# A graph-attention layer on one core: where the steps of a background MLP pass stand among the attention's steps, and how its last groups are cut

## The chip, the cores and the metric

The kernel runs on one core of one Trainium2 chip. The metric is device time in microseconds, the median of three runs. Engines are named as in the profile: PE is TensorE (matmul; PEld its weight load), DVE is VectorE, ACT is ScalarE, POOL is GpSimd, SP is SyncE.

## The reference, cut to what matters

Two residual layers over 6250 nodes of 512 numbers and 100000 edges; an edge takes the key and value of its node `dst` to its node `src`.

```python
x = x + gnn(layernorm(x), [src, dst], edge_attr)     # attention over edges, 8 heads of 64
x = x + ffn(layernorm(x)[None])[0]                    # a small "ALU" per node

# gnn: rows = src, cols = dst of every edge
q, k, v = x @ Wq + bq, x @ Wk + bk, x @ Wv + bv
logits = einsum('ehd,ehd->eh', q[rows] * scale, k[cols]) + att_bias
p = exp(logits - segment_max(logits, rows)[rows])
y = segment_sum(p / segment_sum(p, rows)[rows] * v[cols], rows)
out = y @ Wo + bo

# ffn: decode nibbles of the normalised row, run two three-layer MLPs (160 wide,
# relu after the first two) on them, add one-hot results into columns 128 to 160
```

## The kernel before, in words

A first stage sorts the edges by `src`, normalises the nodes and writes the keys and values of all nodes to DRAM (`kv_d`). The change touches the main loop, which starts some 490 us into the span.

The nodes are sorted by degree and cut into 49 blocks of 128, taken in the order of the list `ORDER`. Block b has `CAP[ORDER[b]]` slots, one slot being one edge of each of its 128 nodes: 34 in the first block, then large and small ones in turn (25, 11, 24, 11, ... 18, 14, ... 16, 16), 10, 9 and 8 in the last three, 804 in all. A block of more than 12 slots is handled in two parts (three in the first two blocks), with a running softmax. Blocks are written here by number and part, 25.1 being the second part of block 25.

A part goes in steps of two slots. For each step:

- GpSimd gathers the keys and values of each slot (`gather`, L110, `kv<-kv_d,rec`) into one of 11 buffers of two slots (`kvp`, `bufs=11`), and, running ahead, the edge records (`rec<-rec_d,eid`): some four gathers a step.
- `pump()` advances background work by one piece: every generator in the list `going`, and the first one in the list `alus`.
- `dots` (L801, L802): VectorE multiplies the keys by the block's queries and sums over each head.
- At the first step of a part, the weighted sum of the *previous* part is issued (`sums`): per step `weigh` multiplies the values by the softmax weights (on VectorE, L812; the second of four on ScalarE in 16 instructions, L810), and TensorE adds the slots up by matmuls with the identity (L1077), two for each slot. These matmuls are the last readers of a `kv` buffer.

After the last step of a part, `softmax` runs on VectorE (L730 to L738), with the exponential on ScalarE (L739); `total` (L754) needs it next.

The list `going` holds a block's own follow-up: `project` (the next block's queries, L790 to L797) and `part_end`, which rescales and adds the part sums (L1041, L1045), divides (L773 to L777), and runs `attend_out`: transposes (L820) and their copy (L823), output projection (L829), and three pumps later the residual and its statistics (L834 to L837, the tile `x1`).

The list `alus` holds the ALU passes of the second layer. A pass covers a group of blocks, four (`GB`) but for the last ones. Its generator `alu` stops (yields) after each of 20 pieces: the root (L842), normalise (L844 to L854), decode (L860 to L873), the transposes `pf` (L878), their copy `fT` (L882), five matmuls of the first layer each with its relu (pm3, L893 and L895), five of the second (pm4, L906 and L908; the fifth sums five weights, the others two), the third layer (p3, L913), a pause, its copy `yf` with a transpose (L917, L921), a pause, and the end (L928 to L963). Finished blocks are scattered to the output by GpSimd (L782).

The program is written under a manual schedule: each engine's queue has the order in which the code issues the instructions. So the place of a `pump()` in the loop is the place of the piece's instructions in the queues of TensorE, ScalarE and VectorE. After the last block, pumps run until nothing is left.

Before, each step has one pump, ahead of its dot products; the weighting of blocks 45 to 48 has one more after every second buffer; the groups are eleven of four blocks (0 to 43), then 44 and 45, 46 and 47, and 48 by itself.

Of the kernel before, what the change touches and what calls it, by code (L numbers as in the profile page):

```python
# [13 lines left out]
AF = mybir.ActivationFunctionType  # L14
# [14 lines left out]
GB = 4  # L29
# [14 lines left out]
def gnn_ffn_kernel(  # L44
# [3 lines left out]
    nc = tc.nc  # L48
# [7 lines left out]
    NB = -(-N // P)  # L56
# [17 lines left out]
    def ctile(shape, name, dt=F32, pool=const):  # L74
        return pool.tile(shape, dt, tag=name, name=name)
# [12 lines left out]
    eps = ctile([P, 1], "eps")  # L88
    nc.vector.memset(eps, EPS)
    warm = ctile([P, 1], "warm")  # L90
# [18 lines left out]
    def gather(dst_t, table, idx):  # L109
        nc.gpsimd.indirect_dma_start(  # L110
            out=dst_t, out_offset=None, in_=table,
            in_offset=bass.IndirectOffsetOnAxis(ap=idx, axis=0))
# [107 lines left out]
    def fetch_keys(b):  # L220
        C = CAP[ORDER[b]]
        t, nbuf = ("0", 1) if b == 0 else ("", LA + 3)
        kg = pre.tile([P, C + 1], F32, tag="kg" + t, name="kg", bufs=nbuf)
        gather(kg, words, pos_i[:, ORDER[b]:ORDER[b] + 1])
        st[b] = dict(kg=kg)
# [18 lines left out]
    def fetch_recs(n, last):  # L244

        while fetched[0] < n and fetched[1] is not None and fetched[1][0] <= last:
            b, s = fetched[1]
            gather(st[b]["rec"][:, s, :], rec_d, st[b]["eid"][:, s:s + 1])
            fetched[:] = fetched[0] + 1, next(wanted, None)
# [501 lines left out]
    def total(lg, cor, den0):  # L751

        den = ap_.tile([P, H], F32, tag="den", name="den", bufs=3)
        nc.vector.tensor_reduce(den, lg.rearrange("p c h -> p h c"), AX.X, OP.add)  # L754
        if cor is not None:
            nc.vector.tensor_tensor(den0, den0, cor, op=OP.mult)
            nc.vector.tensor_tensor(den, den, den0, op=OP.add)
        return den
# [40 lines left out]
    def dots(kvt, n, q, dot, s):  # L799
        k = kvt[:, :n, :D]  # L800
        nc.vector.tensor_tensor(k, k, q[:, None, :].to_broadcast([P, n, D]), op=OP.mult)  # L801
        nc.vector.tensor_reduce(  # L802
            dot[:, s:s + n, :], k.rearrange("p s (h d) -> p s h d", h=H), AX.X, OP.add)

    def weigh(kvt, n, p, p_ps, s, on_act):
        v = kvt[:, :n, D:].rearrange("p s (h d) -> p s h d", h=H)
        if on_act:
            for i in range(n):
                for h in range(H):
                    nc.scalar.mul(v[:, i, h], v[:, i, h], p[:, s + i, h:h + 1])  # L810
        else:
            nc.vector.tensor_tensor(  # L812
                v, v, p_ps[:, s:s + n, :, None].to_broadcast([P, n, H, DK]), op=OP.mult)
# [156 lines left out]
    def fetch_nodes(b):  # L970
        if b - 4 in ends:
            run(ends.pop(b - 4))
        xg = ap_.tile([P, 2 * D], F32, tag="xg", name="xg", bufs=4)
        gather(xg, xx_d, nid[:, b:b + 1])
        st[b]["xg"] = xg


    going = []
    alus = []
# [8 lines left out]
    def store(n=1):  # L988
        for _ in range(n):
            stores.pop(0)[1]()  # L990

    def pump():
        last[1] += 1
        for g in list(going) + alus[:1]:
            if next(g, True):
                for l in (going, alus):
                    if g in l:
                        l.remove(g)
        if stores and stores[0][0] + last[0] <= last[1]:
            store()  # L1000

    def run(g):

        while alus and g in alus and g is not alus[0]:
            run(alus[0])
        for _ in g:
            pass
        for l in (going, alus):
            if g in l:
                l.remove(g)  # L1010
# [8 lines left out]
                LASTR if ORDER[g + j] == NB - 1 else P), g))  # L1019


    heads_of = list(range(0, NB - 5, GB)) + [NB - 5, NB - 3, NB - 1]
    head = {b: max(g for g in heads_of if g <= b) for b in range(NB)}

    def start_group(g):
        i = heads_of.index(g)
        n = (heads_of + [NB])[i + 1] - g
        t, nbuf = ("", 2) if i < len(heads_of) - 2 else (str(i), 1)
        if i > 1 and nbuf > 1 and heads_of[i - 2] in groups:
            run(groups.pop(heads_of[i - 2])[2])  # L1030
            while stores and stores[0][2] <= heads_of[i - 2]:
                store()
        groups[g] = [o2.tile([P, n if t else GB, D], F32, tag="x1" + t, name="x1", bufs=nbuf),
                     o2.tile([P, GB, 2], F32, tag="mv", name="mv", bufs=4), None]

    def part_end(b, i, parts, p_y, cor, den):
        yield
        s_ = st[b]
        if i:
            y = s_["y"]  # L1040
            nc.vector.tensor_tensor(y, y, cor[:, :, None].to_broadcast([P, H, DK]), op=OP.mult)  # L1041
        yield
        yield
        if i:
            nc.vector.tensor_tensor(y, y, heads(p_y), op=OP.add)  # L1045
        else:
            y = s_["y"] = o2.tile([P, H, DK], F32, tag="y", name="y", bufs=2)
            if parts > 1:
                nc.scalar.copy(y, heads(p_y))
        if i < parts - 1:  # L1050
            return
        some = divide(y, y if i else heads(p_y), den, p_y)
        yield
        g = head[b]
        if g == b:
            start_group(g)
        x1, mv, _ = groups[g]
        for _ in attend_out(y, some, s_["xg"], x1[:, b - g], mv[:, b - g]):
            yield
        del st[b]  # L1060
        if b == NB - 1 or head[b + 1] != g:
            groups[g][2] = group_end(g, b - g + 1)
            alus.append(groups[g][2])
# [5 lines left out]
    def sums(b, i, parts, dot, cor, p_ps, kvs, n_):  # L1069
        s_ = st[b]  # L1070
        den = s_["den"] = total(dot, cor, s_.get("den"))

        p_y = ops.tile([P, D], F32, tag="p_y", name="p_y")
        for k, (kvt, n, s) in enumerate(kvs):
            weigh(kvt, n, dot, p_ps, s, k % 4 == 1)
            for j in range(n):
                nc.tensor.matmul(p_y, ident, kvt[:, j, D:], start=(s + j == 0),  # L1077
                                 stop=(s + j == n_ - 1))
            if b > NB - 5 and k % 2:
                pump()  # L1080
        ends[b] = part_end(b, i, parts, p_y, cor, den)
        going.append(ends[b])

# [2 lines left out]
    for b in range(NB):  # L1086
        C = CAP[ORDER[b]]
        s_ = st[b]
        rec, q = s_["rec"], s_["q"]
        parts = -(-C // PART)  # L1090
        m = None
        for i in range(parts):
            s0, s1 = C * i // parts, C * (i + 1) // parts
            n_ = s1 - s0
            dot = ap_.tile([P, n_, H], F32, tag="dot", name="dot", bufs=2)
            kvs = []
            for s in range(s0, s1, 2):
                n = min(2, s1 - s)
                kvt = kvp.tile([P, 2, 2 * D], F32, tag="kv", name="kv")
                for k in range(n):  # L1100
                    gather(kvt[:, k, :], kv_d, rec[:, s + k, 0:1].bitcast(I32))
                kvs.append((kvt, n, s - s0))
                done = sum(SLOTS[:b]) + s + n
                if done > HOLD:
                    last[0] = 1000
                fetch_recs(FIRST + (TOTAL - FIRST) * done // (TOTAL - LAST), b + LA)
                if s == s0 and i == 0:
                    if b + LA + 2 < NB:
                        fetch_keys(b + LA + 2)
                    if b + 1 < NB:  # L1110
                        fetch_nodes(b + 1)
                if s == s0 + 2 and i == 0 and b + 1 < NB:
                    pj = project(st[b + 1]["xg"], st[b + 1])
                    going.insert(0, pj)
                pump()
                dots(kvt, n, q, dot, s - s0)
                if s == s0:
                    for f in waiting:
                        f()
                    waiting.clear()  # L1120
                if s == s0 + 2 and i == parts - 1 and b + LA + 2 < NB:
                    read_keys(b + LA + 2)
            m, cor, p_ps = softmax(dot, rec[:, s0:s1], s_["neg"][:, s0:s1], m)
            waiting.append(partial(sums, b, i, parts, dot, cor, p_ps, kvs, n_))
        if b + 1 < NB:
            run(pj)
    for f in waiting:
        f()
    last[0] = 0
    while going or alus or stores:  # L1130
        pump()
# [145 lines left out]
```

## Time and profile before

| what | value |
|---|---|
| median of three runs | 2687.78 us (2687.76 to 2688.94) |
| profiled execution | 2684.3 us, its span 2682.4 us |
| mean granted TensorE clock | 0.864 |
| busy: PE, PEld, DVE, ACT, POOL | 1988.2, 862.5, 2018.2, 884.8, 1710.2 us |
| DMA | 542.31 MB, 202 GB/s over the span |

Times inside the profiled execution are counted from the start of its span. In a timeline's line stand the start, the duration, the engine, the line of the kernel, the operation, the tile written and the tiles read, and in brackets the idle time of that engine just before it with what ended that idle time. In a line of waits stand the waiting instruction, what it waited for, and the total, the count and the longest. In a table of stretches stand the stretch, its length, busy time and instructions of PE, PEld, DVE, ACT and POOL, the granted TensorE clock, the share of the DMA engines and GB/s.

### The profile page before, as it was taken

What the parts mean: (1) busy time and instruction counts of PE and PEld (TensorE: products, weight loads), DVE (VectorE), ACT (ScalarE), POOL (GpSimd) and SP (SyncE); (2) the same over time, 40 slices, a digit from 0 to 9 for tenths busy, and PEclk for the clock granted to TensorE, in tenths of its full rate; (3) what the DMA queues carried; (4) which work ended last, traced back from release to release, by engine and by line L of the source; (5) the groups of instructions that cost most, each with busy time, mean ns of one, the idle gap of its engine ahead of it and who ended that gap; (6) DMA issues with size and microseconds to landing.
All of it is one profiled execution on the core that took longest, in us unless ns stands there. A gap on an engine that the chain in (4) does not pass through costs nothing.

```text
span 2682.4 us, 20184 instructions
## 1 busy us (share of the span) xinstructions
PE 1988.2 (74%) x4853; PEld 862.5 (32%) x4853; DVE 2018.2 (75%) x3562; ACT 884.8 (33%) x2712; POOL 1710.2 (64%) x1857
## 2 busy tenths in 40 slices
PE   7888799256567658677786677867778777787775
PEld 3444344122223223332332223323333323333333
DVE  9899600469677787878879779798888978889762
ACT  6434242123233233232333323333233232333322
POOL 3011177767777677777776767777777777777610
PEclk9999899678788879888898798988889888898886
DMA  8545244566675667777776767767777777777710
GB/s 279 193 132 185 88 145 128 187 204 217 228 238 190 204 217 233 222 227 223 226 226 201 225 205 228 229 218 229 221 225 229 223 227 229 231 230 233 229 63 20
DMA packets 193965, 542.31 MB, mean 202 GB/s; under 512 B 51831, under 2 KB 53174, under 8 KB 193841
## 3 DMA queue, kind: packets, MB, share of 16 engines
q0 software_dynamic: 154416, 464.27, 55.2%
q1 hardware_dynamic: 39425, 76.67, 8.2%
q8 instruction: 42, 0.69, 0.1%
q14 instruction: 82, 0.67, 0.1%
HBM read 472.60 MB, written 68.22 MB: 202 GB/s over the span
## 4 chain that ended last, share of the span: by engine, by line
PE 35%; DVE 32%; POOL 12%; issue 10%; DMA 6%; ACT 3%; SPq 0%; DVEq 0%; POOLq 0%; ACTq 0%
PE p_y L1077 19%; POOL rec L110 7%; DVE kv L801 7%; DVE dot L802 6%; PE pm L906 4%; DVE kv L812 4%; PE pm L829 4%; POOL kv L110 3%; DMA kv<-kv_d,rec 3%; DVE key L143 3%; DVE key L144 2%; PE pm L457 2%; DMA rec<-rec_d,eid 2%; PE q L796 2%; ACT kv L810 2%
## 5 line engine op out<-in xcount | busy, mean ns | idle before, releaser
L1077 PE MATMUL p_y<-kv,ident 128*128 128x512 f32 x1608 | 849.2, 686 | 458.9 <-DVE kv L812 403.9
L110 POOL DMA_INDIRECT kv<-kv_d,rec x804 | 760.6, 946 | 293.0 <-issue 195.5
L110 POOL DMA_INDIRECT rec<-rec_d,eid x804 | 763.6, 950 | 245.1 <-issue 224.4
L1077 PEld LDWEIGHTS p_y<-kv,ident 128*128 128x128 f32 x1608 | 345.0, 222 | 951.3 <-DVE kv L812 459.4
L801 DVE TENSOR_TENSOR kv<-kv,q 128x1024 f32<-128x1024 f32 (+1 forms) x425 | 490.0, 1153 | 207.2 <-PE q L797 110.3
L802 DVE TENSOR_REDUCE dot<-kv 128x16 f32<-128x1024 f32 (+1 forms) x425 | 493.8, 1162 | 20.0
L810 ACT ACTIVATE kv<-kv,dot 128x64 f32<-128x64 f32 x1648 | 402.6, 335 | 0.2 <-DMA kv<-kv_d,rec 0.2
L812 DVE TENSOR_TENSOR kv<-kv,pp 128x1024 f32<-128x1024 f32 (+1 forms) x317 | 346.9, 1151 | 0.0
L796 PE MATMUL q<-wq,xT 128*128 128x512 f32 x392 | 186.8, 620 | 22.0 <-ACT xT L792 22.0
L829 PE MATMUL pm<-wo,yT 128*128 128x512 f32 x392 | 184.1, 614 | 10.5 <-ACT yT L823 10.5
L457 PE MATMUL pm<-wv,xnT 128*128 128x512 f32 (+1 forms) x392 | 186.9, 617 | 0.0
L457 PE MATMUL pm<-wk,xnT 128*128 128x512 f32 (+1 forms) x392 | 180.0, 600 | 0.0
L792 ACT COPY xT<-tr 128x512 f32<-128x512 f32 x49 | 28.7, 585 | 444.9 <-PE tr L790 444.9
L468 ACT COPY kvt<-pm 128x512 f32<-128x512 f32 (+1 forms) x98 | 56.9, 583 | 235.0 <-PE pm L457 160.4
L739 ACT ACTIVATE dot<-dot 128x64 f32<-128x64 f32 (+6 forms) x91 | 23.7, 260 | 309.0 <-DVE dot L738 308.9
L782 POOL DMA_INDIRECT out_dram<-x,nid x49 | 50.1, 1022 | 114.1 <-issue 77.5
L110 POOL DMA_INDIRECT kg<-sorted_d,pos_i x49 | 47.0, 960 | 110.9 <-DVE ov L699 96.3
L796 PEld LDWEIGHTS q<-wq,xT 128*128 128x128 f32 x392 | 72.8, 195 | 114.6 <-issue 77.1
L829 PEld LDWEIGHTS pm<-wo,yT 128*128 128x128 f32 x392 | 75.0, 196 | 102.7 <-issue 86.3
L895 ACT ACTIVATE h<-pm,b 128x512 f32<-128x512 f32 (+2 forms) x70 | 44.2, 632 | 185.8 <-PE pm L893 185.8
L143 DVE TENSOR_TENSOR key<-key 128x512 f32<-128x512 f32 x143 | 101.6, 710 | 4.8
L823 ACT COPY yT<-tr 128x512 f32<-128x512 f32 x49 | 28.5, 583 | 231.7 <-PE tr L820 231.7
(253 smaller groups left out, 2022.2 us busy)
## 6 DMA issues: line engine op xcount, KB each, us to landing
kv_d<-kvt SPq DMA_DIRECT2D x48, 512.0 KB
rec<-rec_d,eid POOLq DMA_INDIRECT x804, 3.5
kv<-kv_d,rec POOLq DMA_INDIRECT x804, 5.2
xt<-in_x_dram SPq DMA_DIRECT2D x48, 256.0 KB
xx_d<-xt SPq DMA_DIRECT2D x48, 256.0 KB
xx_d<-xn SPq DMA_DIRECT2D x48, 256.0 KB
rec_d<-R SPq DMA_DIRECT2D x3, 882.0 KB
bt<-in_edge_attr_dram SPq DMA_DIRECT2D x3, 686.0 KB
```

The costliest lines, as they stand in the source:

```text
L110: nc.gpsimd.indirect_dma_start(out=dst_t, out_offset=None, in_=table, in_offset=bass.IndirectOffsetOnAxis(ap=idx, axis=0))
L143: nc.vector.tensor_tensor(ov[:, :, 0, :], av[:, :, 0, :], av[:, :, 1, :], op=OP.min)
L457: nc.tensor.matmul(pm[:r], xnT[b][:, c, :r], wkv[nm_][:, c, :], start=(c == 0), stop=(i == 1 and c == KC - 1))
L468: nc.scalar.copy(kvt[:r, i * D:(i + 1) * D], pm[:r])
L796: nc.tensor.matmul(q, xT[:, c, :], wq[:, c, :], start=(c == 0), stop=False)
L801: nc.vector.tensor_tensor(k, k, q[:, None, :].to_broadcast([P, n, D]), op=OP.mult)
L802: nc.vector.tensor_reduce(dot[:, s:s + n, :], k.rearrange("p s (h d) -> p s h d", h=H), AX.X, OP.add)
L810: nc.scalar.mul(v[:, i, h], v[:, i, h], p[:, s + i, h:h + 1])
L812: nc.vector.tensor_tensor(v, v, p_ps[:, s:s + n, :, None].to_broadcast([P, n, H, DK]), op=OP.mult)
L829: nc.tensor.matmul(pm, yT[:, c, :], wo[:, c, :], start=(c == 0), stop=False)
L906: nc.tensor.matmul(pm[:, :nt], w, h1[:, k, :nt], start=(i == 0), stop=(i == len(terms) - 1))
L1077: nc.tensor.matmul(p_y, ident, kvt[:, j, D:], start=(s + j == 0), stop=(s + j == n_ - 1))
```

## The change

- `pump` takes a number n: the first ALU pass is advanced n times, the list `going` still once.
- In the main loop n is 0 at the last step of a part, 2 at its second step, 1 elsewhere.
- In the last three blocks (46 to 48) there is one more pump after the dot products of each step but the first.
- The pumps inside the weighting are gone.
- The last groups are 40 to 43, 44 and 45, and 46 to 48 (the single block 48 has no pass of its own).
- One more root of a dummy tile on ScalarE stands before the last weighting (`warm`).

```diff
-    def pump():
+    def pump(n=1):
+
         last[1] += 1
-        for g in list(going) + alus[:1]:
+        for g in list(going) + (alus[:1] * n):
             if next(g, True):
...
-    heads_of = list(range(0, NB - 5, GB)) + [NB - 5, NB - 3, NB - 1]
+    heads_of = list(range(0, NB - 5, GB)) + [NB - 5, NB - 3]
...
-        t, nbuf = ("", 2) if i < len(heads_of) - 2 else (str(i), 1)
+        t, nbuf = ("", 2) if i < len(heads_of) - 1 else (str(i), 1)
...
                 nc.tensor.matmul(p_y, ident, kvt[:, j, D:], start=(s + j == 0),
                                  stop=(s + j == n_ - 1))
-            if b > NB - 5 and k % 2:
-                pump()
...
-                pump()
+
+                pump(0 if s + 2 >= s1 else 2 if s == s0 + 2 else 1)
                 dots(kvt, n, q, dot, s - s0)
+                if b > NB - 4 and s > s0:
+                    pump()
...
             run(pj)
+    nc.scalar.activation(warm, eps, AF.Sqrt)
     for f in waiting:
         f()
```

## The prediction

> **What bounds the kernel now.** I read the page's busy table first, then the table of stretches of the main loop, the waits of GpSimd and VectorE there, and the timelines around the waits that the change moves.
>
> ```profile
> PE 1988.2 (74%) x4853; PEld 862.5 (32%) x4853; DVE 2018.2 (75%) x3562; ACT 884.8 (33%) x2712; POOL 1710.2 (64%) x1857
> ```
>
> ```profile
> 1060.00:1560.00 500.00, 362.83 (x839) 151.23 (x839) 411.44 (x690) 157.74 (x525) 372.92 (x393) 0.85 0.71 222
> 1560.00:2060.00 500.00, 380.07 (x886) 158.32 (x885) 427.95 (x742) 164.45 (x549) 372.77 (x392) 0.87 0.71 222
> 2540.00:2682.00 142.00, 94.18 (x287) 50.12 (x285) 60.37 (x163) 38.47 (x105) 14.97 (x15) 0.79 0.14 48
> ```
>
> No engine looks full. But GpSimd's gathers start 1.25 us apart (0.95 busy, 0.30 issue), so 393 of them are 491 of the 500 us. GpSimd sets the pace up to its last key/value gather at 2556; 126 us follow without it.
>
> ```profile
> 1411.94 0.95 POOL L110 DMA_INDIRECT xg<-xx_d,nid  x1 [0.30 <-DVE dg L955]
> 1420.34 0.94 POOL L110 DMA_INDIRECT kv<-kv_d,rec  x1 [7.45 <-PE p_y L1077]
> ```
>
> It is late only where it waits for one of the 11 kv buffers to be freed by the weighted-sum matmuls (L1077). Gaps above 0.5 us between 600 and 2540 come to 34.5 us; the largest are 8.4 (at 894), 7.45 (1420), 4.5 (1570), 3.3 (707). Each follows a late VectorE, whose own waits in this stretch are:
>
> ```profile
> DVE den L754 <- ACT dot L739: 91.8, 18, 9.3
> DVE fT L882 <- PE pf L878: 49.2, 8, 8.5
> DVE yf L917 <- PE p L913: 37.1, 4, 12.1
> DVE x L834 <- PE pm L830: 27.5, 11, 3.9
> ```
>
> VectorE is busy 82 to 86% from 1060 to 2060 and hardly waits for gathers there, so a new VectorE wait is paid once the ring's slack is gone. I measure the slack as the time between a buffer's last matmul and the gather that refills it. Its low points: 0.3 at 1758 (a wait already), 4.8 at 1926, 10.0 at 2097, 2.3 at 2260, 2.0 at 2427.
>
> **The change, part by part.** Parts are written block.part, steps counted from 1. An ALU pass has 20 pieces: root, normalise, decode, pf, fT, five pm3, five pm4, p3, pause, yf, pause, end. I wrote out which piece falls on which step, before and after. Pieces per part stay the same away from the end; only their places move: none at a part's last step, two at its second. The second step comes right after the weighting, so TensorE then has a burst of 12 to 24 matmuls queued, and whatever VectorE wants from TensorE there waits for the burst.
>
> *Softmax waits (gain).* The exponential queues on ScalarE behind the last relu of the part. In three-step parts (14.0, 18.0) that relu now stands ahead of the next q projection: 3.7 us less of 5.9 and 6.1; the waits of 2.9 and 3.2 in the parts after them go. In 22.0, 38.0, 42.0: 0.8 less. In 22.1, 38.1, 42.1 it waits for a pm4 of two weights (1.7 us) instead of five (4.3): 2.5 less. In 26.0, 30.0, 34.0: 0.8 less. In 26.1, 30.1, 34.1 one more two-weight pm4 is queued ahead: 1.7 more.
>
> *fT in groups 20, 24, 28 (cost).* Before, pf was at 25.1 step 1, ahead of the burst, and fT at step 2 found it done. Now both are at step 2, behind the burst and behind block 24's output projection (L829), which the same step issues first.
>
> ```profile
> 1663.68 1.01 PE L878 MATMUL pf<-ident,ft 128*8 128x128 f32 x4 [4.12 <-ACT yT L823]
> 1666.32 10.98 PE L1077 MATMUL p_y<-kv,ident 128*128 128x512 f32 x18 [1.62 <-DVE kv L812]
> 1677.13 3.60 PE L829 MATMUL pm<-wo,yT 128*128 128x512 f32 x8
> 1680.57 0.38 PE L830 MATMUL pm<-bo,sT 66*128 66x512 bf16 x1
> ```
>
> ```profile
> 1669.04 0.67 DVE L882 COPY fT<-pf 8x512 f32<-8x512 f32 x1
> 1680.98 0.69 DVE L834 TENSOR_TENSOR x<-pm,xg 128x512 f32<-128x512 f32 x1 [3.35 <-PE pm L830]
> ```
>
> fT was ready at 1669.0. It would come at 1680.95 + 0.8 for pf, 12.7 later, with the step's dot products (three pairs of 2.4 us) and the later steps queued behind it; x1 then comes at 1681.8 + 0.7 + 7.3 = 1689.8 instead of 1681.0. Net 8.8 per group (the fT waits that stand behind a burst already, 4.3 to 8.5 with one pair of 2.4 in between, would give 3.4 to 7.6; I take the group's own rows), and with the softmax terms 8.8 - 0.8 + 1.7 = 9.7.
>
> *yf in groups 16, 32, 36 (cost).* p3 moves from the first step of 23.0, 39.0 and 43.0 to the second.
>
> ```profile
> 2224.14 3.70 PE L906 MATMUL pm<-h,w1ml 128*128 128x512 f32 x8 [0.78 <-ACT h L908]
> 2229.48 4.46 PE L913 MATMUL p<-h,w 128*8 128x512 f32 x10 [0.78 <-ACT h L908]
> 2233.87 7.13 PE L1077 MATMUL p_y<-kv,ident 128*128 128x512 f32 x16
> ```
>
> The five-weight pm4 then takes p3's place ahead of the burst. The relu that released the pm4 at 2224.1 comes 1.7 later, one two-weight pm4 more being queued: pm4 to 2230.3 and its relu to 2230.9, ScalarE's weighting (16 x 0.245) to 2234.8, twelve matmuls of 0.43 to 2240.0, transposes 0.5, p3 4.46: yf at 2245.0 instead of 2238.2, net 6.8, the softmax gain already in it (0 if VectorE were late anyway; 9.5 by the wait of 7.1 at 1401, which has a dot pair of 2.4 more in between).
>
> *yf in groups 4, 8, 12 and 0.* Groups 4 and 8 get yf a part later and lose about 2 and 6.7 us of delay (softmax included), group 12 about 1.6; group 0 waits some 2 us more, as the pm4 of two weights and that of five change places around the burst.
>
> The scatters of finished blocks move by a few steps with their pass; each keeps its 1.3 us of GpSimd's queue, so they are costed at nothing (1.3 if one falls between two gathers that wait).
>
> *What reaches GpSimd.* Groups 8 and 12 take 8.3 off the wait at 1420, which vanishes (-7.4, 0.9 to spare); 1072 loses 0.7; 894 gains 2. Group 16: 6.8 - 0.9 = +5.9. Group 20: 9.7 against 0.3 = +9.4. Group 24: 9.7 against 4.8 = +4.9; of the 4.8 carried, VectorE's gather waits at 1967 to 1985 (3.1) absorb all but 1.7. Group 28: 11.4 against 10.0 = +1.4; of 10.0 the waits at 2129 to 2134 (2.6) leave 7.4. Group 32: 14.2 against 2.3 = +11.9. Group 36: 2.3 + 6.8 against 2.0 = +7.1. Sum +40.6 - 8.1 + 2 = **+34.5 us**.
>
> *The end.* The ten pumps inside the weighting of blocks 45 to 48 give way to eleven after dot products of 46 to 48. Two serial ALU passes (2628.1 to 2650.3 to 2666.5: 22.2 for two blocks, 16.2 for one) become one of three. I take 27.2: VectorE's start 2.75 and end 3.4, TensorE 19 with the first 10 us at half clock, the rest hand-offs. Two more scatters stand before the last, 1.27 each: -38.4 + 27.2 + 2.5 = -8.7. The bounds are 22.2 (nothing for the third block) and 38.4. Block 48's division no longer waits for block 47's projection behind the last burst: the burst's end to the next pass was 22.0, now 17.6 (four two-matmul pieces 3.4, transposes and copies 3.2, projection 4.0, p3 2.3, VectorE 4.7): -4.4. But that burst ends about 7 later: fT's wait at 2582.95 (6.9) goes, while p3 of group 40 falls behind block 46's burst (yf waits about 12), the last exponential stands behind block 47's projection and a relu (2.7), and the early root adds a table load and itself ahead of ScalarE's last weighting:
>
> ```profile
> 2559.72 1.28 ACT L842 ACT_TABLE_LOAD   x1
> 2561.02 0.30 ACT L842 ACTIVATE sd<-mv,eps 128x2 f32<-128x2 f32 x1
> ```
>
> 1.6 us, and the load it replaces (at 2618) was hidden. Together -8.7 - 4.4 + 7 = **-6 us**; bounds -15 and +5.
>
> The Trainium skill ("ScalarE: Activation LUTs", What ACT_TABLE_LOAD costs) speaks against the early root: a switch costs 1.28 us and a drain of 1.38. By it the root would add 3.0, not 1.6, and the sum would be 1.4 higher. The rows here show the load but the next activation 0.02 us after it.
>
> For the last pass this row decides:
>
> ```profile
> 2631.00:2642.00 11.00, 10.49 (x25) 7.15 (x25) 0.41 (x1) 3.38 (x8) 0.17 (x1) 0.51 0.08 29
> ```
>
> After 6 us without matmuls the granted clock stays at 0.51 for about 10 busy us, then is 1.00. "TensorE: Matmul & The Clock Gate" (Part 1) in the skill has full clock after about 3.4 us of sustained work; the pass would then be some 3 us shorter and the sum as much lower. I use the row.
>
> Sum: 2684.3 (the profiled execution, 1.9 over its span) + 34.5 - 6 = 2712.8. The median of the runs is 3.5 higher, so **2716**.
>
> **The rivals.**
> A, faster: the ring hides the moved fT and yf waits. The place is the refill of the buffers freed at 26.0 to 28.0 and 39.1 to 44.0; it decides if VectorE, after the wait, is less than about 5 us behind when it weighs. For it: VectorE idles elsewhere in the same groups, and the largest old waits fall. Against it: the slack of 0.3, 2.3 and 2.0. Price: -8 in the loop, -6 at the end: 2674.
> B, slower still: no slack helps. 3 x 9.7 + 3 x 6.8 = 49.5, + 2, and the end gives nothing: 2739. For it: the old waits at 1570 and 1758; against it: the 10 us at 2097.
> C: ring and end together cancel the added waits, 2688.
>
> **How the numbers follow.** Forecast (2698 to 2728) 0.55, A 0.25, B 0.12, C 0.08. A and part of C are faster, most of C within 0.2% (5 us, about what the runs can tell apart): faster 0.27, same 0.06, slower 0.67. The range of 2674 to 2738 takes in A's centre and B's.
>
> **What would show it.** GpSimd's wait for L1077 grows from 69 to about 105 us; fT waits in every full group, with 10 to 13 us new in groups 20, 24, 28; yf waits of about 10 new in 16, 32, 36; the softmax waits fall by about 20 us; the wait at 1420 is gone; after the last kv gather one ALU pass of about 27 us. I am wrong if the fT and yf waits are there and GpSimd's are not (A), or if the softmax waits fall far more: then their cause was not the queue that I counted.

## The result, and the profile after

The change made the kernel slower. The median of six runs is 2708.27 us (2705.49 to 2708.92), beside 2687.83 us (2686.83 to 2688.94) for six runs of the kernel before: a ratio of 1.0073, 95% interval 1.0062 to 1.0083, or 20.4 us. The profiled execution took 2708.14 us, its span 2706.3 us, and the mean granted clock was 0.865. The forecast was 2716.

In what follows the *loop* is the time from the first key/value gather of the span to the one that opens block 47, and the *end* is the rest of the span from there. The loop went from 2027.6 to 2053.4 us (+25.8), the end from 164.7 to 159.8 (-4.9). That sums to +20.9. The two profiled executions are 23.8 apart, because the first stage, which the change does not touch, took 3.0 us longer in the second one; the medians are 20.4 apart.

The page's busy table after the change:

```profile
PE 1979.2 (73%) x4807; PEld 854.4 (32%) x4807; DVE 2017.1 (75%) x3536; ACT 882.5 (33%) x2702; POOL 1710.7 (63%) x1857
```

GpSimd has as many instructions as before, and VectorE lost 26 (one pass of one block). Nothing here explains 20 us. The table of stretches shows where it comes from:

```profile
1060.00:1560.00 500.00, 370.05 (x862) 154.65 (x861) 411.14 (x691) 159.31 (x530) 378.01 (x399) 0.86 0.70 226
1560.00:2060.00 500.00, 352.19 (x809) 146.70 (x808) 404.96 (x699) 152.60 (x512) 356.02 (x375) 0.84 0.67 213
```

In the first stretch GpSimd issued 399 gathers and scatters where it had issued 393: the wait of 7.45 us at 1420 is down to 0.97. In the second it issued 375 instead of 392, and 17 of them at 1.25 us apiece are 21 us. The timeline of GpSimd has the waits themselves (four of sixteen):

```profile
1421.40 0.94 POOL L110 DMA_INDIRECT kv<-kv_d,rec  x1 [0.97 <-PE p_y L1078]
...
1598.83 0.94 POOL L110 DMA_INDIRECT kv<-kv_d,rec  x1 [12.02 <-PE p_y L1078]
...
1708.15 0.94 POOL L110 DMA_INDIRECT kv<-kv_d,rec  x1 [4.10 <-PE p_y L1078]
...
1944.91 0.94 POOL L110 DMA_INDIRECT kv<-kv_d,rec  x1 [4.49 <-PE p_y L1078]
```

All are waits for a buffer that the weighted-sum matmuls free (L1078 now). Gaps above 0.5 us between 600 and 2540 rose from 34.6 us in twelve to 61.5 us in sixteen. A gap holds 0.3 us of issue even where nothing is waited for; less that in the four more gaps, the difference of 26.9 is the loop's 25.8 to within 0.1 us. The waits of GpSimd and then of VectorE in this stretch:

```profile
POOL kv L110 <- PE p_y L1078: 78.9, 72, 13.4
```

```profile
DVE yf L917 <- PE p L913: 76.6, 7, 14.8
DVE fT L882 <- PE pf L878: 73.3, 11, 11.9
DVE den L754 <- ACT dot L739: 69.6, 17, 8.2
...
DVE x L834 <- PE pm L830: 13.0, 6, 4.0
```

GpSimd's wait for L1078 was 50.6 us there. For VectorE, `yf` rose from 37.1 to 76.6 and `fT` from 49.2 to 73.3, while the softmax (`den`) fell from 91.8 to 69.6 and `x` from 27.5 to 13.0.

How one such wait looks is seen in group 20, first on TensorE, then on VectorE:

```profile
1673.35 9.84 PE L1078 MATMUL p_y<-kv,ident 128*128 128x512 f32 x18 [7.22 <-DVE kv L812]
1683.03 3.60 PE L829 MATMUL pm<-wo,yT 128*128 128x512 f32 x8
1686.47 0.38 PE L830 MATMUL pm<-bo,sT 66*128 66x512 bf16 x1
1686.69 0.60 PE L878 MATMUL pf<-ident,ft 128*8 128x128 f32 x4
```

```profile
1687.33 0.68 DVE L882 COPY fT<-pf 8x512 f32<-8x512 f32 x1 [11.17 <-PE pf L878]
```

The four transposes take 0.6 us and need nothing that the weighted sum's matmuls, the burst, make. They stand behind its 18 matmuls and a projection in TensorE's queue, and VectorE, which has the copy at the head of its own queue, stands still for 11.2 us with the step's own dot products and those of the next steps behind it.

In group 32 the wait is there too, but its cost is not:

```profile
2250.25 0.27 DVE L754 TENSOR_REDUCE den<-dot 128x8 f32<-128x64 f32 x1 [4.75 <-ACT dot L739]
...
2268.70 0.68 DVE L917 COPY yf<-p 8x512 f32<-8x512 f32 x1 [9.78 <-PE p L913]
```

Before, this `yf` did not wait at all, and that `den` waited 8.22:

```profile
2229.60 0.27 DVE L754 TENSOR_REDUCE den<-dot 128x8 f32<-128x64 f32 x1 [8.22 <-ACT dot L739]
...
2238.20 0.67 DVE L917 COPY yf<-p 8x512 f32<-8x512 f32 x1
```

GpSimd lost 1.5 us there, where the forecast had 11.9.

At the end, the tail of ScalarE's queue ahead of the last weighting, the last part of the burst that follows on TensorE, and the clock in the last pass:

```profile
2632.56 0.47 ACT L895 ACTIVATE h<-pm,b 128x256 f32<-128x256 f32 x1 [4.47 <-PE pm L893]
2632.93 0.25 ACT L739 ACTIVATE dot<-dot 128x64 f32<-128x64 f32 x1
2633.21 0.22 ACT L743 COPY pp<-dot 128x64 f32<-128x64 f32 x1
2633.44 1.28 ACT L1129 ACT_TABLE_LOAD   x1
2634.74 0.20 ACT L1129 ACTIVATE warm<-eps 128x1 f32<-128x1 f32 x1
2634.84 3.92 ACT L810 ACTIVATE kv<-kv,dot 128x64 f32<-128x64 f32 x16
```

```profile
2638.81 4.56 PE L1078 MATMUL p_y<-kv,ident 128*128 128x512 f32 x10 [0.78 <-ACT kv L810]
```

```profile
2662.00:2667.00 5.00, 3.51 (x7) 1.69 (x8) 1.15 (x6) 1.56 (x3) 0.97 (x1) 0.50 0.30 108
2667.00:2676.00 9.00, 9.00 (x18) 4.46 (x17) 0.00 (x0) 3.49 (x6) 0.00 (x0) 0.62 0.00 0
```

The last dot products ended at 2627.51, but the exponential started at 2632.93, behind a relu whose matmul had stood behind block 47's projection. And the last pass opens at half clock.

### The profile page after: what moved, and what is told of

Its sections match the earlier page's. It is cut to its first block, busy times and chain, and to the rows that moved or that the text cites. A ratio compares the mean times of both kernels' runs of the same rounds, so it can differ in the third digit from the quotient of the medians.

```text
span 2706.3 us, 20055 instructions
## 1 busy us (share of the span) xinstructions
PE 1979.2 (73%) x4807; PEld 854.4 (32%) x4807; DVE 2017.1 (75%) x3536; ACT 882.5 (33%) x2702; POOL 1710.7 (63%) x1857
## 4 chain that ended last, share of the span: by engine, by line
DVE 35%; PE 31%; issue 12%; POOL 12%; DMA 6%; ACT 3%; SPq 0%; DVEq 0%; POOLq 0%
PE p_y L1078 16%; DVE kv L801 9%; POOL rec L110 7%; DVE dot L802 6%; DVE kv L812 5%; DMA kv<-kv_d,rec 4%; PE pm L906 4%; POOL kv L110 3%; DVE key L143 3%; PE pm L829 3%; DVE key L144 2%; PE pm L457 2%; ACT kv L810 2%; DMA rec<-rec_d,eid 2%; PE q L796 1%
## 5 line engine op out<-in xcount | busy, mean ns | idle before, releaser
L1078 PE MATMUL p_y<-kv,ident 128*128 128x512 f32 x1608 | 849.6, 686 | 499.5 <-DVE kv L812 430.5
L1078 PEld LDWEIGHTS p_y<-kv,ident 128*128 128x128 f32 x1608 | 344.9, 222 | 992.8 <-DVE kv L812 482.2
L792 ACT COPY xT<-tr 128x512 f32<-128x512 f32 x49 | 28.7, 586 | 440.2 <-PE tr L790 440.2
L823 ACT COPY yT<-tr 128x512 f32<-128x512 f32 x49 | 28.6, 584 | 236.7 <-PE tr L820 236.6
L457 PEld LDWEIGHTS pm<-wv,xnT 128*128 128x128 f32 (+1 forms) x392 | 76.4, 198 | 85.5 <-issue 83.5
```

The costliest lines, as they stand in the source:

```text
L457: nc.tensor.matmul(pm[:r], xnT[b][:, c, :r], wkv[nm_][:, c, :], start=(c == 0), stop=(i == 1 and c == KC - 1))
```

## The experiments

The theory: the loop pays for VectorE's copies of TensorE results (`fT`, `yf`) that now stand behind a weighted-sum burst, and GpSimd passes the delay on wherever the ring of 11 buffers has no slack. The end gains by one pass for two. The rivals: the ring has nothing to do with it, the regrouping itself costs, or the end loses. Every ratio is to runs of the kernel before that were made beside the run in question; their medians are 2688.5, 2690.9 and 2689.0 us, so two experiments are compared by their ratios or their traces.

**The end alone, and the loop alone.** The kernel after, with one pump a step up to block 44:

```diff
-                pump(0 if s + 2 >= s1 else 2 if s == s0 + 2 else 1)
+                pump(1 if b <= NB - 5 else 0 if s + 2 >= s1 else 2 if s == s0 + 2 else 1)
```

> The loop up to block 44 as before, everything from block 45 on as in the changed kernel. Theory (the moved pieces cost the loop 25 to 28 us, the new end gains about 5): 2683, between 2680 and 2687. Rival L (the end is where the time went): 2700 or more. Rival N (the end gives nothing): 2688.

Measured: 2679.48 us, ratio 0.9963 (0.9952 to 0.9975). The loop took 2027.5 us, as before, and the end 156.3. GpSimd's waits from 600 to 2540 are those of before (50.6 there):

```profile
POOL kv L110 <- PE p_y L1078: 49.9, 61, 8.3
```

Then the converse, the kernel before with the new places up to block 44 only:

```diff
-                pump()
+                pump(1 if b > NB - 5 else 0 if s + 2 >= s1 else 2 if s == s0 + 2 else 1)
```

> The changed pattern of pumps (none at a part's last step, two at its second) up to block 44, groups and end as before. Theory: before plus the loop's 26, so 2713, between 2708 and 2718, with GpSimd's wait for the weighted-sum matmuls between 600 and 2540 at about 61 us, against 34.5 before. Rival L (the end is where the time went): within 5 us of 2688.

Measured: 2717.12 us, ratio 1.0111 (1.009 to 1.0131). The loop is 2053.3 and its list of waits is that of the kernel after (12.0 at 1597, 4.2 at 1706, 4.5 at 1943, and so on):

```profile
POOL kv L110 <- PE p_y L1077: 78.9, 73, 13.4
```

So the change is two changes of opposite sign, -9.1 and +28.6 us against the kernel before, whose sum of 19.5 is close to the 20.4 of both. The loop also makes the old end 6.4 us longer (171.1 instead of 164.7); 5.6 of them are GpSimd's wait for a buffer in block 48, 14.6 instead of 9.0.

**The groups alone.** The kernel before, with the last groups 44 and 45, and 46 to 48:

```diff
-    heads_of = list(range(0, NB - 5, GB)) + [NB - 5, NB - 3, NB - 1]
+    heads_of = list(range(0, NB - 5, GB)) + [NB - 5, NB - 3]
```

> The kernel before with the last groups alone changed: 40 to 43, 44 and 45, 46 to 48, all pumps where they were. Theory (one pass of 27 to 28 us and two more scatters take the place of passes of 22.2 and 16.2): 8 to 9 us less than before, so 2679 to 2680. Rival P (the end gains by the moved pumps, not by the groups): within 2 us of before.

Measured: 2681.2 us, ratio 0.9969 (0.9957 to 0.998), the end 158.0. The regrouping gives nearly all of the end's gain (-6.7 of -8.4 us in the profiled runs); moving the pumps out of the weighting, with the early root (1.5 us, below), adds little.

**The fT wait taken away.** In groups 20, 24 and 28 the decode and the transposes `pf` are one piece, so that `pf` stands a step earlier, and a pause after `fT` keeps every later piece in its place:

```diff
-        yield
+        if not early:
+            yield
         pf = ops.tile([P, D], F32, tag="tr", name="pf", bufs=1)
...
+        if early:
+            yield
```

> The changed kernel, but in groups 20, 24 and 28 pf stands in one piece with decode, so ahead of the burst again, with a pause after fT in its place. Theory (the wait for fT behind the burst makes VectorE late, and what exceeds the ring's slack makes GpSimd late): the three waits of 11.1 to 11.9 go, GpSimd's waits of 10.9, 5.0 and 5.1 in these groups fall to about 3, 0 and 0, and the time falls by 17 (14 to 21) to about 2691. Rival D (VectorE is the bound, its waits count one for one): 3 x 8.8 = 26 less, 2682. Rival H (these waits are hidden): 2708.

Measured: 2683.77 us, ratio 0.9986 (0.9974 to 0.9999), some 24 us less than the kernel after. GpSimd's and VectorE's waits from 600 to 2540:

```profile
POOL kv L110 <- PE p_y L1081: 58.3, 69, 13.8
```

```profile
DVE fT L883 <- PE pf L879: 41.1, 8, 7.5
```

The three waits are gone (73.3 us in 11 became 41.1 in 8), and so are all of GpSimd's from 1700 on but 3.1 and 0.7 us, also those of groups 32 and 36, which this edit did not touch. The theory had 14 to 21 us less, and the loop gave 20.6; the time itself lies nearer to the rival's 2682, so this run alone does not decide between them (the one with a buffer less does). In groups 32 and 36 the copies of `yf` still wait 9.8 and 11.5 us, and GpSimd waits 0 and 0.7: a refill of part 39.1 has 3.6 us more slack than in the kernel after (20.9, 17.3), one of 43.1 2.3 more. So much came over from group 28.

**The yf wait taken away.** `yf` two pieces later in group 16, one piece in 32 and 36, at a place where the burst is over (one of the pauses behind it goes instead):

```diff
+            for _ in range(late):
+                yield
             nc.vector.tensor_copy(yf[:, t0:t1], p3[:, :nt])
...
-        yield
+        if not late:
+            yield
...
-        for _ in alu(x1, mv, n):
+        for _ in alu(x1, mv, n, {16: 2, 32: 1, 36: 1}.get(g, 0)):
```

> The changed kernel, but yf comes later in groups 16 (two pieces), 32 and 36 (one piece), at the first step of the next part. Theory: the waits of 11.2, 9.8 and 11.5 go; GpSimd's wait of 12.0 at 1599 falls to 0 to 2, those of 1.5 and 3.1 in groups 32 and 36 to 0; the time falls by 15 (12 to 18) to about 2693. Rival D (one for one): 32 less, 2676. Rival H (hidden): 2708.

Measured: 2684.03 us, ratio 0.9987 (0.9978 to 0.9997), some 24 us less than the kernel after.

```profile
POOL kv L110 <- PE p_y L1081: 61.4, 71, 13.8
```

```profile
DVE yf L919 <- PE p L913: 48.0, 6, 14.8
```

The 12.0 us at 1599 and those at 2285 and 2455 are gone (the copies in groups 32 and 36 still wait 1.7 us each), and the loop is 18.6 shorter, at the upper bound of the theory's 12 to 18. The time as a whole, 24 less, lies outside that range, midway to the 32 of rival D. A further 5.4 came in the end, where GpSimd's gap in block 48 fell from 11.3 to 5.8 us (9.0 before the change), which the theory had not counted.

The two edits together give 39.2 in the loop, more than the 25.8 that the change added. That is no contradiction: the second also removes 6.9 us that the kernel before had at 1570 and 1592, and both remove the 4.6 us of groups 32 and 36, which are the price of two delays that together exceed the slack. Less these, 27.7 us are left, beside the 28.7 that groups 16 to 36 lost by the change.

**One buffer less.** The kernel after with 10 key/value buffers:

```diff
-    kvp = ctx.enter_context(tc.tile_pool(name="kvp", bufs=11, **main))
+    kvp = ctx.enter_context(tc.tile_pool(name="kvp", bufs=10, **main))
```

> The changed kernel with 10 kv buffers instead of 11. Theory (a late VectorE costs what exceeds the ring's slack): the slack falls by one step of four gathers, 5.0 us; each excursion of the lag that starts from an idle VectorE (near 610, 710, 800, 900, 1070, 1420) costs up to 5 more, later ones nothing more until the lag has been worked off: 25 us slower (15 to 40), 2733. Rival D (VectorE is the bound of the loop, GpSimd's waits are only its shadow): within 3 us of 2708.

Measured: 2743.11 us, ratio 1.0198 (1.0185 to 1.0212), some 33 us slower than the kernel after on this measure.

```profile
POOL kv L110 <- PE p_y L1078: 114.7, 75, 14.4
```

VectorE's `fT` and `yf` waits are about as long as with 11 (69.8 and 73.4 us), but GpSimd's waits for the ring are 36 us longer. The loop is 42.3 us longer and the end 4.7 shorter. The time is inside the theory's range of 15 to 40, above its 25, and far from the rival's 3: the ring's slack sets what a wait of VectorE costs; a ring of 12 was not tried.

**No early root.** The kernel after without the dummy root:

```diff
-    nc.scalar.activation(warm, eps, AF.Sqrt)
     for f in waiting:
         f()
```

> The changed kernel without the early root (warm). Theory, by the rows: ScalarE's last weighting starts 1.6 us earlier and the table is loaded later, while ScalarE waits: 1.6 less than the changed kernel. Rival, by the skill's price of a switch with its drain: 3.0 less. Rival W (the early root pays): 1 to 2 more.

Measured: 2706.03 us, ratio 1.0061 (1.0048 to 1.0074); the difference to 1.0073 is inside the intervals, so the trace must tell. From the start of the last exponential to the end of the last burst it was 10.44 us and is 8.97, and the table load now lies in a pause of ScalarE:

```profile
2631.35 0.25 ACT L739 ACTIVATE dot<-dot 128x64 f32<-128x64 f32 x1
...
2647.01 1.28 ACT L842 ACT_TABLE_LOAD   x1
```

By these two traces the early root costs 1.5 us, the theory's figure and not the rivals' 3.0 less or 1 to 2 more.

**The pump after block 48's last dot products.** The exponential waits behind it; here it is left out:

```diff
-                if b > NB - 4 and s > s0:
+                if b > NB - 4 and s > s0 and (b < NB - 1 or s + 2 < s1):
                     pump()
```

> The kernel after, but without the pump after the last step's dot products of block 48 (one of the eleven that the change added). In the kernel after, that pump issues block 47's output projection (3.7 + 0.4 us of TensorE) and a two-matmul piece with its relu; the last softmax's exponential queues on ScalarE behind that relu and starts 5.4 us after the last dot products, 1.3 in the kernel before. Theory: the two sides of this pump cancel. The exponential, the weighting and the last burst come 4.1 us earlier, but the projection (4.1 us) and the piece (0.7) then stand on TensorE behind the burst, ahead of block 48's own transposes: the burst's end to the division of the last pass's statistics grows from 16.7 to about 21, as it was 21.9 before. Time 2708 to 2709, 0 to +1 us. Rival: the projection fits into TensorE's pauses while VectorE divides and ScalarE copies (some 3 us), and the earlier exponential is a gain: 2704 to 2705.

Measured: 2708.8 us, ratio 1.0069 (1.0045 to 1.0093). No difference from the kernel after can be told, but the interval is wider than the 4 us between theory and rival, so only the trace speaks, and it is of the slowest of the four executions (2704.4 to 2712.5). The exponential starts 1.32 us after the last dot products instead of 5.42 (4.1 won), and the burst's end to the last pass grew from 16.7 to 19.8 (3.2 lost, about 4 forecast), so most of the projection stands in the way behind the burst, as it did ahead of it. Beyond that, the exponential to the burst's end is 1.3 us longer, at half clock, and the last pass 1.5. The burst here, its first five us, and the same two for the kernel without the early root:

```profile
2633.19 9.92 PE L1078 MATMUL p_y<-kv,ident 128*128 128x512 f32 x16 [3.23 <-DVE kv L812]
```

```profile
2633.20:2638.20 5.00, 5.00 (x6) 2.17 (x7) 2.19 (x2) 4.01 (x17) 0.00 (x0) 0.50 0.00 0
```

```profile
2633.16 7.16 PE L1078 MATMUL p_y<-kv,ident 128*128 128x512 f32 x16 [2.21 <-DVE kv L812]
```

```profile
2633.20:2638.20 5.00, 5.00 (x12) 2.26 (x13) 4.07 (x8) 2.50 (x11) 0.00 (x0) 1.00 0.00 0
```

Sixteen equal matmuls took 9.92 and 7.16 us; the granted clock was 0.50 in the first five of the one and 1.00 in those of the other.

**All pieces at their better places.** One pump a step as in the first experiment; decode and `pf` in one piece in every pass, with the pause after `fT`; `yf` later in groups 0, 4, 8 and 12. Inside `alu` the edits are those shown for `fT` and `yf`, with `pf` early in every group; the line that says where `yf` comes later:

```diff
...
-        for _ in alu(x1, mv, n):
+        for _ in alu(x1, mv, n, {0: 3, 4: 2, 8: 2, 12: 2}.get(g, 0)):
```

> One pump at every step up to block 44, the changed end, and in every pass pf in one piece with decode (a pause after fT in its place), yf three pieces later in group 0 and two later in groups 4, 8 and 12. Theory: of GpSimd's 34.5 us of waits in the loop those at 894, 1420, 1570 and 1758 go (about 25), the end gives 8 as in the kernel with the changed end alone: 2655, between 2648 and 2664. Rival S (softmax waits of 92 us, which stay, keep VectorE just as late): 2679.

Measured: 2661.36 us, ratio 0.9893 (0.988 to 0.9905): faster than both kernels. The loop is 2004.1 us, 23.5 less than before, and GpSimd's waits for the ring from 600 to 2540:

```profile
POOL kv L110 <- PE p_y L1081: 36.4, 59, 8.7
```

The 8.7 is in block 48, past the loop; in the loop no gap above 4.3 us is left. The softmax waits are still 89.3 us, so rival S has fallen. The end, 159.5 us, gave 5.3 and not 8: beside the 156.3 of the kernel with the changed end alone, the projection ahead of the last exponential took 5.40 instead of 3.70 us, the last burst 10.09 instead of 8.64 and the last pass 29.3 instead of 27.8, the first two at a granted clock that fell to 0.50; the last dot products ended 1.3 us earlier after the opening of block 47. Last, this kernel without the early root (the same edit as above):

> The fastest kernel so far (the early end with no ALU piece fewer in the loop, decode and pf in one piece and a pause after fT, yf a few pieces later in groups 0, 4, 8 and 12) without the early root ahead of the last weighting. By the run without it on the kernel after, ScalarE's last weighting starts 1.5 us earlier, and the table load lies in a wait of ScalarE: 1.5 us less than that kernel, ratio to the kernel before 0.9888 instead of 0.9893, 2660 us; the Trainium skill's switch cost of 1.28 and a drain of 1.38 (page ScalarE: Activation LUTs, What ACT_TABLE_LOAD costs) would make it 2.9 less, 2658.5. A rival: nothing, if the load is then on the path ahead of the last pass's root.

Measured: 2657.6 us, ratio 0.988 (0.9861 to 0.9899), not to be told from 0.9893. ScalarE's load has moved into a pause,

```profile
2598.80 1.28 ACT L842 ACT_TABLE_LOAD   x1
```

and its weighting starts 0.42 instead of 1.91 us after the exponential, yet the exponential to the burst's end is 11.87 us, as it was 11.89. Both bursts ran at a granted clock of 0.50 in their first five us and took 10.1 us without a pause, so that TensorE, not ScalarE, set their end:

```profile
2573.59 5.40 PE L829 MATMUL pm<-wo,yT 128*128 128x512 f32 x8 [0.57 <-ACT yT L823]
...
2582.04 10.07 PE L1081 MATMUL p_y<-kv,ident 128*128 128x512 f32 x16 [2.21 <-DVE kv L812]
```

In these traces the early root's 1.5 us were to be had only where the burst ran at full clock.

## Why the prediction was right, and where it was off

**Direction and mechanism.** Each sign named under "What would show it" is there. GpSimd's wait for the weighted-sum matmuls is 100.5 us over the whole span (forecast about 105, before 69.2). `fT` waits 11.2, 11.1 and 11.9 us in groups 20, 24 and 28 (10 to 13). `yf` waits 11.2, 9.8 and 11.5 in 16, 32 and 36 (about 10). The softmax waits fell by 22.2 (20), though not all in the places named: the waits of 2.9 and 3.2 in the parts after 14.0 and 18.0, which were to go, are 2.6 and 3.1, and larger gains in 22.1, 38.1 and 42.1 (3.4 to 3.5 each instead of 2.5) and in some first parts made up for them. That the total came out is in part luck. Of the 7.45 at 1420 0.97 is left, 0.3 of it issue. Taking the copies' waits away gave the loop's time back, which shows the cause; rival A has fallen. Rival B has too: the end alone gains 8.4 us, and groups 32 and 36 paid little. C's 2688 is 20 us off. (B's 2739 lay 1 us outside the range that was to take it in.)

**The loop's sum** was 34.5 forecast, 26.9 measured in the same gaps. By place:

| place | forecast | measured |
|---|---|---|
| 600 to 800 | 0 | +0.5 |
| 894 (`yf` of group 0) | +2 | +5.0 |
| 1072 | -0.7 | -0.7 |
| 1420 | -7.4 | -6.5 |
| group 16 | +5.9 | +5.1 |
| group 20 | +9.4 | +8.9 |
| group 24 | +4.9 | +5.0 |
| group 28 | +1.4 | +5.1 |
| group 32 | +11.9 | +1.5 |
| group 36 | +7.1 | +3.1 |

Groups 16, 20 and 24 came out within 1 us, terms that were read from the group's own rows. Four are off. Group 0's `yf` wait went from 9.9 to 14.8, which is 4.9 and not "some 2". In group 28 the delay that came over from group 24 was 4.4 us (the slack at gather step 33.1, 19.1 before, was 14.7) instead of the 1.7 that 3.1 us of VectorE's gather waits were to leave of it. Only 2.0 of those 3.1 are waits for gathers, and these went; the rest is a wait for the root (`sd`) on ScalarE, and it grew from 1.15 to 2.12:

```profile
1983.48 0.18 DVE L844 RECIPROCAL sd<-sd 128x4 f32<-128x4 f32 x1 [1.15 <-ACT sd L842]
```

```profile
2006.36 0.18 DVE L844 RECIPROCAL sd<-sd 128x4 f32<-128x4 f32 x1 [2.12 <-ACT sd L842]
```

The largest miss is group 32, in both its terms. Of the "7.4" carried over from group 28 3.6 arrived, by the kernel with `pf` early; the wait of 3.3 us for the root at 2150 went along with the gather waits. And the "net 6.8" of `yf` was nothing: in that kernel, where nothing is carried, the refill at the low point of 2260 has 2.7 us of slack, and 2.3 before. The forecast had this case in brackets ("0 if VectorE were late anyway") and priced the other. With 3.6 carried the 2.3 were used up and GpSimd waited 1.2 us more than its issue. In group 36 the carried 2.3 was right, and of its 6.8 2.1 arrived (the slack of 2.0 used up, 0.4 of waiting).

The step that failed is that I counted only the softmax waits as giving way, 0.8 and 2.5 us in such a group. In group 32, up to the refill at the low point, VectorE's waits for results sum to 20.8 us before and 21.6 after: the new 9.8 of `yf` stands against 4.1 less for the softmax, 3.3 for the root (`sd`) and 1.7 for `fT`. A VectorE that is late can find results of other engines done, and I let only its gather waits absorb a delay; the root's wait in group 24, which grew, shows that not each of them gives way. The misses on both sides, +8.2 and -15.7 by place, partly cancel, so that the sum is nearer than its terms.

**The end** was -6 forecast and -4.9 measured. The one pass took 27.8 us (27.2) and opened at a granted clock of 0.50 from 2662.9 to about 2674, as the row of before had it (0.51 for about 10 us). The Trainium skill's 3.4 us ("TensorE: Matmul & The Clock Gate", Part 1) do not agree with this pass. Burst's end to the last pass: -5.2 (-4.4). The burst's end itself came 8.4 later (about 7): +6.1 to the last dot products, +4.1 for the exponential behind the relu (2.7 forecast), -1.8 for the weighting and the burst. Among these is the early root, 1.5 us in the kernel where its removal showed (1.6 forecast); against it stands the clock, which the forecast did not have for the burst: it opened at 1.00 after a pause of 2.21 us, and at 0.50 after one of 6.68 before, and it took 8.64 instead of 10.43 us. The drain of 1.38 that the skill adds to a switch ("ScalarE: Activation LUTs", What ACT_TABLE_LOAD costs) is not seen: the next activation starts 0.02 us after the load, and leaving both out won 1.5.

**To the median.** The forecast added 3.5 us because the profiled execution of before was that far below its median. Adding it was right, since the profiled execution after (2708.14) is at its own median. The difference may lie in the first stage, which took from 489.4 to 493.1 us in the twelve profiled executions (490.2 before, 493.1 after); the executions behind the medians were not profiled, so this is not shown.

## What to carry to other kernels

A copy from TensorE's results belongs either ahead of the weighted-sum burst's matmuls or well behind them: at the step after the weighting it costs the rest of the burst (10 to 12 us here), however small its own work, with all that the waiting engine has queued behind it. Whether that reaches the end is read from the slack of the ring at that place, the time between a buffer's last reader and its refill; it is paid once the slack is used up, and a delay carried from one group to the next can be paid down by any wait of the late engine on the way, not by its waits for data alone. Test the two halves of such a change apart: here -9 us stood hidden behind +29, and the changed end, with one pump a step in the loop and single pieces moved away from the burst, gave a kernel 1.1% faster (interval 0.95 to 1.2%).

## What the hardware showed that I had not expected

The same burst of 16 matmuls, after a pause of TensorE of 2.2 to 3.2 us, took 7.16 us in one kernel and 9.9 to 10.1 us in three others, the granted clock in its first five us being 1.00 or 0.50. The length of the pause does not tell them apart: 2.21 us stood ahead of the burst at full clock, and also ahead of two of those at half clock. In these two the eight matmuls of the projection before it, after a pause of 0.57 us, had already taken 5.40 us, with a granted clock of 0.57 and 0.54 from 2575 to 2578; after the same pause they took 3.70 in the kernel at full clock. What tells them apart was not settled. At the end of a kernel it can hide a gain of 1 to 3 us.
